# First block of a fused attention and expert kernel: row chunks split in pairs, engine order written by hand

## The chip, the cores and the metric

The kernel runs on 1 core of one Trainium2 chip. The metric is the device time of one execution in microseconds (us). The median of 3 runs of the kernel before is 2581.15 us (2580.57 to 2585.92).

## The reference

The input x is 2 x 2048 tokens of 2048 features. Each token is normalised, and the result goes into an attention layer with one head of width 512 and into a feed-forward layer of 64 gated experts of rank 8; both results are added to x.

```python
xn = _layernorm(x, axis=-1)                       # no weight, no bias
# attention
q, k, v = split(xn @ Wqkv + bqkv)                 # 3 x 512 columns
out_a = softmax(q @ k.T / sqrt(512)) @ v @ Wo + bo
# experts
scores = (xn @ Wq_w.T) @ keys.T                   # 16 router columns, 64 experts
gate = softmax over the 16 greatest scores, 0 elsewhere
z = (xn @ A_w.T) * gate, each gate over its 8 columns
out_f = z @ B_w.T * 2
x = x + out_a + out_f
```

Everything is float32. TensorE multiplies a rounded form (fp32r), so each operand is kept as a high part (the value rounded to fp32r) and a low part (the value minus its high part), and each product is three matmuls: high times high, high times low, low times high.

## The kernel before, in words

Tokens are worked on in blocks of T = 512, a block in NT = 4 rows of 128 tokens; a row's 2048 features are NCH = 16 chunks of 128. The later blocks are read already transposed (xT), are normalised by statistics that were gathered beside other work, and go through matrix products with fewer multiplications (phases P1 to P7). The first block has nothing to hide behind, so it is made from x itself, in `first_block` (L319):

- `load` (L328) reads a row of 128 tokens into two tiles of 128x1024. `normal` (L338) takes four statistics of 512 columns each on VectorE (L225), merges them (L228), makes the negative mean nm (L341) and the variance plus epsilon ve (L218) on VectorE, and 1/sqrt on GpSimd (rs, L219). `scale` (L344) normalises three quarters of the row on VectorE (L349) and the last on ScalarE, in two operations (L353, L354).
- `turn` (L356) transposes the row's 16 chunks on TensorE (L363), four to a PSUM bank, in the banks acc 0, 1, 2 and 6. From each bank ScalarE writes four high parts (`split_hi`, L127) and VectorE four low parts (`split_lo`, L130), chunk by chunk: 128x128 each.
- `piece` and `low` (L396, L399) load the eight pieces of the values' weight wv[0] (two chunks by VH = 264 columns each; 16 of these columns are the router's) and split them: high parts on ScalarE, low parts on VectorE, and on GpSimd for pieces 2, 3 and 4.
- `mul` (L375) multiplies one row by one piece, in 6 matmuls of 128x264, so that a row takes 48. The row's sums lie in the banks acc 3, 4, 5 and 6. Within a product the order of PASSES (L59) is low x with high w, high x with low w, then high with high.
- The loop over the rows t issues `scale` of the row t + 1 ahead of the third piece, `normal` of the row t + 2 behind it, and `turn` of the row t + 1 ahead of the seventh. Then `values_out` (L291) splits the results and stores them, and a second half does the same with wv[1], now piece by piece over all four rows.

The scheduler of the recording layer sets each engine's final order from its own estimates; `behind(...)` (L117) makes an instruction come after a named earlier one of its engine. In the built program VectorE so mixes the rows: statistics of the row t + 2 lie between the low parts of the row t + 1, and weight parts are put in between. On SP's queue stand, in this order: half of row 0, 5 weight pieces, row 1, 3 pieces, rows 2 and 3, six small constants, then the second half's first four pieces and the q weights (wq).

The results of the split, xn, are read twice more: by `features` (L867), which multiplies all chunks with wq (x is then the moving operand, 512 wide), and by `whole` (L1135), which adds high and low parts to the normalised block again, where the next phases need it (L1140, 128x512 each). Where the chunks lie is set by XH0 and XH1 (L178): one 128x1024 slot for each chunk, which holds its high part and its low part; one chunk lies in two half slots. The slots are the later homes of other tiles (GROUPS and T_SLOTS).

TensorE starts with 25 matmuls on zeros in the bank misc, the eighth bank, which later serves small transposes.

Of the kernel before, what the change touches and what calls it, by code (L numbers as in the profile page):

```python
# [62 lines left out]
def attn_ffn_kernel(ctx: ExitStack, tc, x, xT, wq, wv, wob, bqk, bv, bo, keysT, out):  # L63
# [114 lines left out]
    XH0 = [s for n in range(3) for s in (GROUPS[3][n + 1], T_SLOTS[n])] + [26, T_SLOTS[3]]  # L178
    XH1 = [s for n in range(3) for s in (GROUPS[2][n + 1], T_SLOTS[4 + n])] + [None, T_SLOTS[7]]

    def split_room(at):
        if at is None:
            return [half(k)([P, T], FR, "xh") for k in (7, 8)]
        t = big(at)([P, 2, T], FR, "xh")
        return [t[:, k, :] for k in range(2)]
# [133 lines left out]
    def first_block(steps):  # L319
# [3 lines left out]
        xn = [split_room(at) for at in XH0 + XH1]  # L323
        rows, mv = {}, const.tile([P, NT, 2], F32, name="mv", bufs=2)
        rs = const.tile([P, NT], F32, name="rs")
        nm = const.tile([P, NT], F32, name="nm")

# [10 lines left out]
        def normal(t):  # L338
            st = const.tile([P, 4, 6], F32, name="st6", bufs=2)
            row_stats(mv[:, t, :], rows[t], 0, st)  # L340
            last["nm"] = nc.vector.tensor_scalar(nm[:, t : t + 1], mv[:, t, 0:1], -1.0, None, ALU.mult)  # L341
            rstd(rs[:, t : t + 1], mv[:, t, 1:2], 1)

        def scale(t):  # L344
            for n in range(4):
                c, h = divmod(n, 2)
                v = rows[t][c][:, h * 512 : (h + 1) * 512]
                if n < 3:
                    last["row"] = nc.vector.tensor_scalar(  # L349
                        v, v, mv[:, t, 0:1], rs[:, t : t + 1], ALU.subtract, ALU.mult  # L350
                    )
                else:
                    nc.scalar.activation(v, v, AF.Identity, bias=nm[:, t : t + 1])  # L353
                    last["mul"] = nc.scalar.mul(v, v, rs[:, t : t + 1])  # L354

        def turn(t, g0=0, g1=NCH // 4):  # L356
            sl = slice(t * P, (t + 1) * P)
            for g in range(g0, g1):
                pt = acc((0, 1, 2, 6)[g])
                for j in range(4):  # L360
                    c = 4 * g + j
                    k = (c % 8) * P
                    nc.tensor.transpose(pt[:, j * P : (j + 1) * P], rows[t][c // 8][:, k : k + P], ident)  # L363
                for part in range(2):
                    for j in range(4):
                        hi, lo = (xn[4 * g + j][a][:, sl] for a in range(2))
                        pj = pt[:, j * P : (j + 1) * P]
                        if part == 0:
                            split_hi(hi, pj)
                        else:  # L370
                            last["row"] = split_lo(lo, pj, hi)

        r_w0 = Ring(sb, "h0", "h1", "h2", "h3", "B25", "B34", "B35", "B32")

        def mul(ps, wh, t, c2):  # L375
            sl = slice(t * P, (t + 1) * P)
            for cc in range(2):
                c = 2 * c2 + cc
                product(
                    ps[:, :VH], lambda a: xn[c][a][:, sl], lambda b: wh[:, b, cc, :],  # L380
                    c == 0, c == NCH - 1,
                )
# [5 lines left out]
        for j in range(25):  # L388
            nc.tensor.matmul(pw, warm[:, :P], warm, start=True, stop=True)
        load(0, 512)  # L390
        normal(0)
        scale(0)

        wh = []

        def piece():  # L396
            wh.append(wv_hi(0, len(wh), r_w0))

        def low(n):  # L399
            with behind("row", "nm", "mul"):  # L400
                wh[n] = weights_lo(*wh[n], nc.gpsimd if 2 <= n < 5 else None)

        piece()
        piece()
        low(0)
        low(1)
        piece()
        turn(0, 0, 2)
        low(2)
        piece()  # L410
        turn(0, 2, 4)
        low(3)
        piece()
        low(4)
        load(1, 1024)
        for n in range(5, N2):
# [1466 lines left out]
```

## Time and profile before

| what | value |
|---|---|
| median of 3 runs | 2581.15 us (2580.57 to 2585.92) |
| span of the profiled execution | 2582.2 us |
| TensorE busy | 2556.8 us, 99% |
| VectorE busy | 1981.2 us, 77% |
| ScalarE busy | 926.9 us, 36% |
| GpSimd busy | 560.8 us, 22% |
| mean granted TensorE clock | 0.998 |
| DMA | 615.41 MB, mean 238 GB/s |

The page gives the profiled execution by its span, from the first to the last instruction; it has no other time of that execution, so its span stands beside the runs. The profile is of one execution. A group is shown by line, engine and operation, with the tile that it writes, an arrow and the tiles that it reads; "idle before" is the time for which its engine stood still ahead of it, with what ended that. Matmul ends are modelled: starts are the better measure. The clock is a share of full speed.

### The profile page before, as it was taken

To read this page: it belongs to the slowest core of one execution; us is meant where nothing else is said; L and a number is where in the kernel's file an instruction comes from. 1 tells how busy PE (TensorE), PEld (TensorE's weight loads), DVE (VectorE), ACT (ScalarE), POOL (GpSimd) and SP (SyncE) were. 2 spreads that over 40 slices of the span, in tenths; PEclk is the share of its full clock that TensorE was granted. 3 is DMA by queue.
4 is the path that set the end of the run, shared out by engine and by line. 5 is a ranking of instruction groups with operands and counts; after the bars stand their busy time and mean duration, and the time that the engine had idled before them with its cause. 6 is when DMAs were issued, how large, how long until landed. Compare 5 with 4: busy or idle time off the path is not lost. (4 is left out here: it accounts for less than half of the span.)

```text
span 2582.2 us, 34227 instructions
## 1 busy us (share of the span) xinstructions
PE 2556.8 (99%) x12546; PEld 2159.7 (84%) x12546; DVE 1981.2 (77%) x2692; ACT 926.9 (36%) x1327; POOL 560.8 (22%) x340
## 2 busy tenths in 40 slices
PE   9999999999999999999999999999999999999999
PEld 8897888888888889888887878878878888888887
DVE  7788997867778678777668768688597777797675
ACT  4333333232332323343345446354364222332221
POOL 2382310001000000000000000000013565576654
PEclk9999999999999999999999999999999999999999
DMA  8988964668356673678899798898897554665552
GB/s 297 311 300 276 354 224 144 227 212 274 125 176 225 211 250 120 201 269 270 315 310 309 240 338 278 282 324 290 277 320 265 182 162 157 203 200 179 167 168 101
DMA packets 334297, 615.41 MB, mean 238 GB/s; under 512 B 28409, under 2 KB 151345, under 8 KB 334129
## 3 DMA queue, kind: packets, MB, share of 16 engines
q1 hardware_dynamic: 318864, 583.33, 67.2%
q10 hardware_dynamic: 15264, 29.89, 3.3%
q8 instruction: 99, 1.62, 0.3%
q14 instruction: 70, 0.57, 0.1%
HBM read 457.76 MB, written 155.35 MB: 237 GB/s over the span
## 5 line engine op out<-in xcount | busy, mean ns | idle before, releaser
L135 PE MATMUL acc<-t,pw 128*128 128x512 f32 x3744 | 859.0, 390 | 6.4 <-DVE t L130 4.7
L135 PEld LDWEIGHTS acc<-t,pw 128*128 128x128 f32 x3744 | 699.8, 188 | 153.9 <-DVE t L130 6.4
L1629 PE MATMUL acc<-wb,s 128*128 128x512 f32 x2688 | 609.6, 389 | 0.0
L1629 PEld LDWEIGHTS acc<-wb,s 128*128 128x128 f32 x2688 | 504.4, 188 | 105.0 <-DVE s L130 0.2
L1613 POOL TENSOR_TENSOR xo<-xo,bo_bc 128x512 f32<-128x512 f32 x128 | 213.5, 1675 | 884.5 <-DMA bo_bc<-in_bo 592.3
L127 ACT CAST pw<-pw 128x1024 fp32r<-128x1024 f32 (+1 forms) x218 | 230.5, 1058 | 442.1 <-PE acc L135 287.8
L135 PE MATMUL acc<-ph,vt 128*128 128x512 f32 x1536 | 376.7, 390 | 0.3 <-ACT ot L1474 0.2
L130 DVE TENSOR_TENSOR pw<-pw 128x1024 fp32r<-128x1024 f32 (+1 forms) x218 | 288.7, 1324 | 95.9 <-ACT pw L127 94.3
L135 PEld LDWEIGHTS acc<-ph,vt 128*128 128x128 f32 x1536 | 287.7, 188 | 62.1 <-issue 1.2
L1335 PE MATMUL acc<-qt,kt 128*128 128x512 f32 x1344 | 333.9, 390 | 2.6 <-ACT sp L1345 1.5
L1335 PEld LDWEIGHTS acc<-qt,kt 128*128 128x128 f32 x1344 | 250.9, 188 | 58.9 <-DVE qt L130 2.2
L135 PE MATMUL acc<-pw,t 128*128 128x264 f32 x2400 | 295.9, 285 | 2.9 <-DVE pw L130 0.9
L135 PEld LDWEIGHTS acc<-pw,t 128*128 128x128 f32 x2400 | 294.2, 189 | 5.3 <-ACT pw L127 1.1
L127 ACT CAST s<-xz 128x1024 fp32r<-128x1024 f32 x112 | 118.0, 1054 | 375.1 <-PE acc L1629 300.3
L130 DVE TENSOR_TENSOR s<-xz,s 128x1024 fp32r<-128x1024 f32 x112 | 177.8, 1589 | 41.0 <-ACT s L127 41.0
L130 DVE TENSOR_TENSOR t<-xq,t 128x1024 fp32r<-128x1024 f32 x108 | 141.9, 1321 | 24.3 <-ACT t L127 24.1
L535 POOL TENSOR_TENSOR zt<-zt,g 128x512 f32<-128x512 f32 x28 | 44.6, 1603 | 516.0 <-DMA g<-gd 274.6
L127 ACT CAST t<-xq 128x1024 fp32r<-128x1024 f32 x108 | 113.1, 1051 | 114.1 <-DVE xq L667 59.6
L1618 DVE TENSOR_TENSOR xo<-xo,acc 128x512 f32<-128x512 f32 x128 | 86.9, 680 | 52.1 <-POOL xo L1659 25.2
L127 ACT CAST ph<-sp 128x512 fp32r<-128x512 f32 x128 | 79.4, 620 | 109.4 <-PE acc L135 108.5
L1654 POOL TENSOR_TENSOR xo<-xo,u 128x512 f32<-128x512 f32 x64 | 111.5, 1772 | 21.5 <-DVE u L1652 21.4
L225 DVE BATCH_NORM_STATS2 st<-xs 128x6 f32<-128x512 f32 x128 | 85.0, 683 | 39.5 <-DMA xs<-in_x 39.2
(174 smaller groups left out, 2229.4 us busy)
## 6 DMA issues: line engine op xcount, KB each, us to landing
vt<-v_d SPq DMA_DIRECT2D x128, 512.0 KB, 5.4
kt<-kp_d SPq DMA_DIRECT2D x224, 256.0 KB, 5.7
pw<-sq_d SPq DMA_DIRECT2D x96, 512.0 KB, 4.3
pw<-in_wq SPq DMA_DIRECT2D x72, 512.0 KB, 3.7
xo<-in_x SPq DMA_DIRECT2D x128, 256.0 KB, 3.0
xz<-oz_d SPq DMA_DIRECT2D x64, 512.0 KB, 4.4
out_y<-xo SPq DMA_DIRECT2D x128, 256.0 KB, 2.6
xq<-in_xT SPq DMA_DIRECT2D x56, 512.0 KB, 5.1
```

Source lines behind the costliest of these rows:

```text
L127: return nc.scalar.copy(hi, src)
L130: return (eng or nc.vector).tensor_tensor(lo, src, raw(hi), ALU.subtract)
L135: last["pe"] = nc.tensor.matmul(ps, st(a_), mv(b_), start=first and n == 0, stop=end and n == 2, skip_group_check=more,)
L225: nc.vector.bn_stats(st[:, parts, :], xt[:, h * 512 : (h + 1) * 512])
L535: nc.gpsimd.tensor_tensor(zt, zt, gx[n], ALU.mult)
L1335: last["pe"] = nc.tensor.matmul(ps, st[:, d, a, :], mv[c][:, d, :], start=not more and d == 0 and i == 0, stop=d == 1 and i == 2, skip_gro ...
L1613: nc.gpsimd.tensor_tensor(xs, xs, bo_bc[q // (NB // 2 * NH), c], ALU.add)
L1618: nc.vector.tensor_tensor(xs, xs, ps, op)
L1629: nc.tensor.matmul(ps, st[a_][:, kk, sl], mv[b_], start=not more and kk == 0 and n == 0, stop=kk == ND - 1 and n == 2, skip_group_check=more,)
L1654: nc.gpsimd.tensor_tensor(xo[q, t, a, 1], xo[q, t, a, 1], v, ALU.add)
```

## The change

Chunks go in pairs. A slot of 128x1024 now holds the high parts of two neighbouring chunks, or the low parts of two, so that one instruction of 128x2x128 splits two chunks out of a PSUM bank: 8 casts on ScalarE for a row instead of 16, and on VectorE 7 paired subtractions and, for the last pair, whose low parts lie in two half slots, 2 single ones. `whole` adds a pair at a time (128x1024) likewise.

The order in the first half is written out: `inline` puts each instruction behind the one issued before it on its engine (VectorE, ScalarE, TensorE). All loads of the block are issued first; SP's order stays as it was. High parts of the weights follow each bank's casts; low parts of the pieces 2, 4 and 6 are on GpSimd, those of 0, 1, 3, 5 and 7 on VectorE. In `normal` the variance comes ahead of nm. Each product begins with high times high. Transposes of a row's first two banks stand ahead of the previous row's last piece, those of the other two behind it; the fourth bank is misc instead of acc 6.

In the built program VectorE's order is, from the first row's scaling on: low part of piece 0; four chunks; piece 1; four chunks; piece 3; eight chunks; piece 5; statistics of row 1; piece 7; scaling of row 1; twelve chunks of row 1; statistics of row 2; the last four chunks of row 1; scaling of row 2; and so on. ScalarE's, after its first weight cast: the last quarter of row 0 (two operations); piece 1; four chunks; pieces 2 and 3; four chunks; piece 4; four chunks; piece 5; four chunks; pieces 6 and 7; row 1. TensorE's: 16 transposes, 42 matmuls, 8 transposes, 6 matmuls, 8 transposes, 42 matmuls, and so on. Behind the first block the engines' orders are the same but for some neighbouring places between 140 and 210 us, where `whole` stands among other steps.

```diff
-    XH0 = [s for n in range(3) for s in (GROUPS[3][n + 1], T_SLOTS[n])] + [26, T_SLOTS[3]]
-    XH1 = [s for n in range(3) for s in (GROUPS[2][n + 1], T_SLOTS[4 + n])] + [None, T_SLOTS[7]]
+    XH0 = [(GROUPS[3][n + 1], T_SLOTS[n]) for n in range(3)] + [(26, T_SLOTS[3])]
+    XH1 = [(GROUPS[2][n + 1], T_SLOTS[4 + n]) for n in range(3)] + [(T_SLOTS[7], None)]
...
+        def inline(key, f, *a, **k):
+            if key in tail:
+                with tc.issue_after(tail[key].ins):
+                    tail[key] = f(*a, **k)
+            else:
+                tail[key] = f(*a, **k)
+            return tail[key]
...
         def normal(t):
             st = const.tile([P, 4, 6], F32, name="st6", bufs=2)
-            row_stats(mv[:, t, :], rows[t], 0, st)
-            last["nm"] = nc.vector.tensor_scalar(nm[:, t : t + 1], mv[:, t, 0:1], -1.0, None, ALU.mult)
-            rstd(rs[:, t : t + 1], mv[:, t, 1:2], 1)
+            for k in range(4):
+                c, h = divmod(k, 2)
+                dve(nc.vector.bn_stats, st[:, k, :], rows[t][c][:, h * 512 : (h + 1) * 512])
+            dve(nc.vector.bn_aggr, mv[:, t, :], st)
+            ve = const.tile([P, NT], F32, name="ve", bufs=2)
+            dve(nc.vector.tensor_scalar, ve[:, :1], mv[:, t, 1:2], EPS, None, ALU.add)
+            nc.gpsimd.tensor_tensor(rs[:, t : t + 1], ve[:, :1], nhalf[:, :1], ALU.pow)
+            dve(nc.vector.tensor_scalar, nm[:, t : t + 1], mv[:, t, 0:1], -1.0, None, ALU.mult)
...
+        def turn(t, g):
+            pt = turned[t, g] = acc(g) if g < 3 else misc()
+            for j in range(4):
+                c = 4 * g + j
+                k = (c % 8) * P
+                pe(nc.tensor.transpose, pt[:, j * P : (j + 1) * P], rows[t][c // 8][:, k : k + P], ident)
+
+        def sides(t, g, part):
+            sl = slice(t * P, (t + 1) * P)
+            for cp in (2 * g, 2 * g + 1):
+                src = turned[t, g][:, (cp % 2) * 2 * P : (cp % 2 + 1) * 2 * P]
+                src = src.rearrange("p (k t) -> p k t", k=2)
+                hi, lo = xn[cp]
+                if part == 0:
+                    act(split_hi, hi[:, :, sl], src)
+                elif isinstance(lo, list):
+                    for k in range(2):
+                        dve(split_lo, lo[k][:, sl], src[:, k, :], hi[:, k, sl])
+                else:
+                    dve(split_lo, lo[:, :, sl], src, hi[:, :, sl])
...
+                for n, (a, b) in enumerate(PASSES[::-1]):
...
+        wload(5)
+        load(1, 1024)
+        wload(3)
+        load(2, 1024)
+        load(3, 1024)
+        normal(0)
+        high()
         scale(0)
-        wh = []
-        def piece():
-            wh.append(wv_hi(0, len(wh), r_w0))
-        def low(n):
-            with behind("row", "nm", "mul"):
-                wh[n] = weights_lo(*wh[n], nc.gpsimd if 2 <= n < 5 else None)
...
+        high()
         low(0)
+        for g in range(4):
+            turn(0, g)
+            sides(0, g, 0)
+            sides(0, g, 1)
+            high()
+            if g == 0:
+                low(1)
+                high()
+            if g == 1:
+                low(2)
+                low(3)
+            if g == 3:
+                low(4)
+                low(5)
+                high()
+        low(6)
+        constants()
+        ps = [acc(3 + t) for t in range(NT)]
         for t in range(NT):
-            ps.append(acc(3 + t))
             for c2 in range(N2):
-                if t + 1 < NT and c2 == 2:
-                    scale(t + 1)
-                    if t + 2 < NT:
-                        with behind("row"):
-                            normal(t + 2)
-                if t == 0 and c2 == 4:
-                    low(6)
-                    low(7)
-                    load(3, 1024)
-                    constants()
-                if t + 1 < NT and c2 == 6:
-                    with behind("pe"):
-                        turn(t + 1)
+                if t + 1 < NT and c2 == 0:
+                    normal(t + 1)
+                    if t == 0:
+                        low(7)
+                    else:
+                        sides(t, 3, 1)
+                    scale(t + 1)
+                if t + 1 < NT and c2 == N2 - 1:
+                    turn(t + 1, 0)
+                    turn(t + 1, 1)
                 mul(ps[t], wh[c2], t, c2)
+            if t + 1 < NT:
+                for g in range(4):
+                    if g > 1:
+                        turn(t + 1, g)
+                    sides(t + 1, g, 0)
+                    if g < 3 or t + 2 == NT:
+                        sides(t + 1, g, 1)
...
     def whole(ch, cp):
         t = big(GROUPS[3 - ch][cp])([P, 2, T], F32, "xq")
-        for k in range(2):
-            hi, lo = xn[ch * HC + 2 * cp + k]
-            nc.vector.tensor_tensor(t[:, k, :], raw(hi), raw(lo), ALU.add)
+        hi, lo = xn[(ch * HC) // 2 + cp]
+        if isinstance(lo, list):
+            for k in range(2):
+                nc.vector.tensor_tensor(t[:, k, :], raw(hi[:, k, :]), raw(lo[k]), ALU.add)
+        else:
+            nc.vector.tensor_tensor(t, raw(hi), raw(lo), ALU.add)
```

## Prediction

> **What bounds the kernel now.** I read the page first, then TensorE's timeline over the first 45 us, then VectorE's, then busy time and granted clock in stretches.
>
> ```profile
> span 2582.2 us, 34227 instructions
> ...
> PE 2556.8 (99%) x12546; PEld 2159.7 (84%) x12546; DVE 1981.2 (77%) x2692; ACT 926.9 (36%) x1327; POOL 560.8 (22%) x340
> ```
>
> TensorE has work 99% of the time; over the whole span it is idle for 2582.2 - 2556.8 = 25.4 us. A change that keeps its matmuls can only win idle time, and time at a low clock. The change touches the first block, so I look there (TensorE; start, length, group, idle before):
>
> ```profile
> 9.29 1.91 PE L363 MATMUL acc<-ident,xs 128*128 128x128 f32 x16
> 12.01 3.31 PE L135 MATMUL acc<-wh,xh 128*128 128x264 f32 x25 [0.81 <-DVE xh L130]
> 15.63 1.00 PE L135 MATMUL acc<-wh,xh 128*128 128x264 f32 x6 [0.31 <-POOL wh L130]
> 18.51 0.88 PE L135 MATMUL acc<-wh,xh 128*128 128x264 f32 x5 [1.89 <-DVE wh L130]
> 19.52 2.98 PE L363 MATMUL acc<-ident,xs 128*128 128x128 f32 x16
> 22.15 0.57 PE L135 MATMUL acc<-wh,xh 128*128 128x264 f32 x1
> 23.00 6.33 PE L135 MATMUL acc<-wh,xh 128*128 128x264 f32 x47 [0.28 <-DVE xh L130]
> 29.17 1.91 PE L363 MATMUL acc<-ident,xs 128*128 128x128 f32 x16
> 30.83 6.09 PE L135 MATMUL acc<-wh,xh 128*128 128x264 f32 x48
> 36.77 1.91 PE L363 MATMUL acc<-ident,xs 128*128 128x128 f32 x16
> 38.43 1.71 PE L135 MATMUL acc<-wh,xh 128*128 128x264 f32 x12
> 41.52 3.68 PE L135 MATMUL acc<-wh,xh 128*128 128x264 f32 x28 [1.38 <-DVE xh L130]
> ```
>
> From start to start, 16 transposes take 30.83 - 29.17 = 1.66 us (0.104 each) and 48 matmuls 36.77 - 30.83 = 5.94 (0.124 each): 7.60 us a row of tokens. The first half of the values so ends at 41.52 + 48 x 0.124 = 47.45. The waits sum to 0.81 + 0.31 + 1.89 + 0.28 + 1.38 = 4.67 us. VectorE stands behind nearly all of them:
>
> ```profile
> 11.66 3.26 DVE L130 TENSOR_TENSOR xh<-acc,xh 128x128 fp32r<-128x128 f32 x16 [0.86 <-ACT xh L127]
> 14.84 2.46 DVE L225 BATCH_NORM_STATS2 st<-xs 128x6 f32<-128x512 f32 x4
> 17.33 0.26 DVE L228 BATCH_NORM_AGGREGATE mv<-st 128x2 f32<-128x24 f32 x1
> 17.63 0.15 DVE L341 TENSOR_SCALAR nm<-mv 128x1 f32<-128x1 f32 x1
> 17.70 0.14 DVE L218 TENSOR_SCALAR ve<-mv 128x1 f32<-128x1 f32 x1
> 17.76 0.70 DVE L130 TENSOR_TENSOR wh<-ws,wh 128x528 fp32r<-128x528 f32 x1
> 18.91 1.46 DVE L349 TENSOR_SCALAR xs<-xs,mv,rs 128x512 f32<-128x512 f32 x3 [0.46 <-POOL rs L219]
> ```
>
> From the second row's first statistics (14.84) to its scaling (18.91) are 4.07 us, and 0.61 more to its first transpose. The stretches (TensorE's busy time is the first after the colon, the clock follows POOL) show the price of the hole at 16.6 to 18.5:
>
> ```profile
> 16.86:20.27 3.41, 1.63 (x12) 1.37 (x13) 2.88 (x8) 1.51 (x3) 0.96 (x1) 1.00 0.75 276
> 20.27:23.68 3.41, 3.13 (x16) 2.80 (x15) 3.41 (x11) 3.27 (x17) 0.22 (x1) 0.51 0.78 232
> ```
>
> TensorE was busy for 1.63 of 3.41 us, and the next 3.41 us had half the clock: 1.7 us lost.
>
> **The change part by part.** *Paired splits.* A row has 16 high casts on ScalarE and 16 subtractions on VectorE; now 8 casts, and 7 paired plus 2 single subtractions. Neither trace row is 2x128 wide. ScalarE: 2.81 / 16 = 0.176 for one of 128; a 128x256 copy out of PSUM later in the trace takes 0.38 alone, less the 0.10 by which neighbours overlap (a cast of 128 lasts 0.28 to 0.33): 0.28. Bounds 0.25 and 2 x 0.176 = 0.35. VectorE: 2.85 / 14 = 0.204 for 128, 1.05 / 3 = 0.35 for 248; I take 0.36, bounds 0.35 and 2 x 0.204 = 0.41 (above it lies the 512-wide row, 0.68 alone, some 0.61 in a chain). A row: ScalarE 8 x 0.28 = 2.24 for 2.81, VectorE 7 x 0.36 + 2 x 0.204 = 2.93 for 3.25.
>
> [...]
>
> *Row 0.* SP's loads stand in the same order, so statistics end as before; the variance now goes ahead of nm: scaling 0.08 earlier, 8.03 to 9.49. On ScalarE the row's last quarter is scaled before the second weight cast, which ends near 9.92. Then by the built order, with 0.58 per weight cast (1.16 / 2): high pairs at 9.92, two weight casts, pairs at 11.64, a cast, pairs at 12.78, a cast, pairs at 13.92. VectorE must see both casts of a bank: 0.28 + 0.38 = 0.66 after each of these starts. Its chain, 0.65 a weight subtraction (1.32 / 2): weight 0 to 10.14; wait to 10.58, two pairs to 11.28; weight 1 to 11.93; wait to 12.30, pairs to 13.0; weight 3 to 13.65, pairs to 14.35; wait to 14.58, a pair and two singles to 15.33; weight 5 to 15.98. Only then come the second row's statistics: 15.98 for 14.84, since two weight subtractions (1.3) stand ahead of them and the pairing repays little. The first transpose of row 1 so comes at 15.98 + 4.07 + 0.61 - 0.08 = 20.6 us (before 19.52).
>
> *TensorE meanwhile.* High times high goes first, so its start at 11.2 replaces 12.01; it follows the pieces (13.7 for piece 3, 16.0 for piece 5) and has done 42 matmuls by 17.5; the order by hand now puts the transposes next. It stands 3.1 us: one hole instead of two. I let the following 3.4 us run at half clock as the row shows: from 20.6 to 23.7, 1.6 us lost.
>
> [...]
>
> *Rows 1 to 3.* What is left at 20.6: 48 transposes and 150 matmuls, 48 x 0.104 + 150 x 0.124 = 23.6 us. Is VectorE quick enough? From a row's first transpose: third bank at 0.83 + 0.74 = 1.57, its subtractions at 1.57 + 0.63 (transpose to cast, 37.40 - 36.77) + 0.66 = 2.86, done 3.56; the next row's statistics to 6.02; variance and GpSimd's power 1.23 (GpSimd 0.55 beside PSUM work), in which the last bank's 0.76 are hidden; scaling and first transpose 0.6: 7.85. TensorE needs 7.60, so 0.25 is lost at each of two rows. End: 20.6 + 23.6 + 1.6 + 0.5 = 46.3, say 46.2 with roundings. Before: 47.45. **Gain 1.25 us.** The eighth bank (misc) costs nothing: its old readers, the casts and subtractions of the row before, are done 5 us ahead. The waits of 1.38 at the last row and 0.28 go; what is late next is the scaling.
>
> *The second half* begins at 46.2. Its first weight cast follows the last row's casts at about 43.3 (before 42.56), its subtraction ends near 44; needed at 46.2. SP's wq loads that wait for row 3's slots, and the v_d and weight loads queued behind them, come up to 1.5 us later, while the need is 1.2 earlier. The tightest piece is subtracted by 61.2 and needed at 65.2: 4 us less 2.7 leave it hidden; without that cover each microsecond late is one lost.
>
> *Features.* xn's slots change their content; TensorE's instructions do not. Rebuilding rows takes 7 x 1.21 + 2 x 0.64 = 9.75 us of VectorE for 16 x 0.64 = 10.24, beside a busy TensorE: nothing. Near 200 us the weight subtraction that TensorE waits for (1.72 us at 204.3) moves ahead of one 0.42 us operation: 0.15 taken, bounds 0 and 0.42.
>
> Sum: -1.25 - 0.15 = -1.4. The page gives the profiled execution's span alone, 2582.2, which lies 1.05 above the median 2581.15 of runs from 2580.57 to 2585.92. 2582.2 - 1.4 = 2580.8, less 1.05: **2579.7 us**.
>
> **Rivals.** *Given back* (0.22): between 150 and 300 us TensorE is idle for 1.13 + 4.74 + 1.45 = 7.3 us behind VectorE, which has waited for DMA. If that chain keeps its time, the gain ends there: 2581.2. For it: DMA shares of 0.87 to 0.95 from 50 to 200. Against: most of its issues follow TensorE's progress.
> *More than forecast* (0.16): no slow clock (-1.6), and half of those 7.3 us vanish with the new order: 2579.7 - 1.6 - 3.6 = 2574.5. Against: nothing removes work there.
> *Slower* (0.15): the paired subtraction with its strided ends costs more than two single ones. Each 0.1 above 0.36 adds 0.7 to the start of row 1 and to each of two loops, 2.1 in all; from 0.42 the block loses. At 0.61, the 512-wide row's, it ends 5.2 later, and holes of 2 us a row bring another slow stretch (1.7): 2579.7 + 6.9 = 2586.6. For it: VectorE is the bound, no row shows the form. Against: 128 and 248 lie on one line.
> That the order does not come out is excluded by the built program.
>
> **Chances.** Forecast 0.47, given back 0.22, more 0.16, slower 0.15. A measurement tells about 0.2% (5.2 us) from no change: below 2576.0 lies most of "more", 0.14; above 2586.3 most of "slower", 0.11; within 0.75. Range from near the one to near the other: 2575.0 to 2585.5.
>
> **What would show it.** One TensorE hole of about 3 us before row 1's transposes near 20.6, a half clock behind it, no wait over 0.5 later, the first half's end near 46.2, 2x128 subtractions at 0.36 a step, VectorE without a rest. Wrong if the end lies beyond 47.5 or before 44.5, or if the stage at 195 to 262 moves by more than a microsecond against the start.

## The result, and the profile after

| | before | changed |
|---|---|---|
| median of 16 runs each | 2583.15 us (2580.17 to 2586.44) | 2587.64 us (2580.16 to 2592.32) |
| profiled execution: span | 2582.2 us | 2584.3 us (its time 2586.1) |
| mean granted clock, profiled execution | 0.998 | 0.997 |

The changed kernel takes 1.0016 times as long, 95% interval [1.0009, 1.0022], about 4 us more where a gain of 1.4 us, to 2579.7 us, was forecast. A second set of runs gave 1.0018 [1.0009, 1.0027].

Two lines of the page of the changed kernel (span; busy time, share and instructions of each engine):

```profile
span 2584.3 us, 34175 instructions
...
PE 2559.1 (99%) x12546; PEld 2161.9 (84%) x12546; DVE 1975.9 (76%) x2657; ACT 924.2 (36%) x1295; POOL 546.7 (21%) x340
```

VectorE lost 35 instructions and 5.3 us, ScalarE 32 and 2.7 us: the change did what it says. TensorE did not get its work sooner. Its timeline in the first block (start, length, group, idle before and its releaser):

```profile
10.97 1.10 PE L338 MATMUL acc<-wh,xh 128*128 128x264 f32 x7
13.09 3.48 PE L338 MATMUL acc<-wh,xh 128*128 128x264 f32 x24 [1.02 <-DVE wh L130]
17.36 1.60 PE L338 MATMUL acc<-wh,xh 128*128 128x264 f32 x11 [0.79 <-DVE wh L130]
21.95 1.74 PE L338 MATMUL acc<-ident,xs 128*128 128x128 f32 x8 [3.00 <-issue]
...
31.47 1.13 PE L338 MATMUL acc<-ident,xs 128*128 128x128 f32 x8
...
39.44 1.13 PE L338 MATMUL acc<-ident,xs 128*128 128x128 f32 x8
...
41.93 18.26 PE L338 MATMUL acc<-wh,xh 128*128 128x264 f32 x148
```

One hole of 3.0 us stands ahead of row 1's transposes, as forecast, but it ends at 21.95 instead of 20.6. The last row's matmuls start at 41.93, so the first half ends at 41.93 + 48 x 0.124 = 47.9: 0.4 later than before, not 1.25 earlier. VectorE in that time, and then GpSimd:

```profile
5.48 1.88 DVE L338 BATCH_NORM_STATS2 st<-xs 128x6 f32<-128x512 f32 x3 [0.40 <-DMA xs<-in_x]
...
11.26 1.78 DVE L130 TENSOR_TENSOR wh<-ws,wh 128x528 fp32r<-128x528 f32 x1
12.96 0.74 DVE L130 TENSOR_TENSOR xh<-acc,xh 128x256 fp32r<-128x256 f32 x2
13.62 1.16 DVE L130 TENSOR_TENSOR wh<-ws,wh 128x528 fp32r<-128x528 f32 x1
14.71 0.74 DVE L130 TENSOR_TENSOR xh<-acc,xh 128x256 fp32r<-128x256 f32 x2
15.37 0.80 DVE L130 TENSOR_TENSOR xh<-misc,xh 128x256 fp32r<-128x256 f32 x3
16.10 1.21 DVE L130 TENSOR_TENSOR wh<-ws,wh 128x528 fp32r<-128x528 f32 x1
17.23 2.46 DVE L338 BATCH_NORM_STATS2 st<-xs 128x6 f32<-128x512 f32 x4
```

```profile
11.15 1.32 POOL L130 TENSOR_TENSOR wh<-ws,wh 128x528 fp32r<-128x528 f32 x1 [2.29 <-ACT wh L127]
12.77 1.45 POOL L130 TENSOR_TENSOR wh<-ws,wh 128x528 fp32r<-128x528 f32 x1 [0.29 <-ACT wh L127]
15.41 1.33 POOL L130 TENSOR_TENSOR wh<-ws,wh 128x528 fp32r<-128x528 f32 x1 [1.19 <-ACT wh L127]
```

The paired subtractions take 0.37 each. But VectorE's weight subtractions, priced at 0.65, took 1.78, 1.16 and 1.21 wherever one of GpSimd's ran at the same time. Statistics of row 1 start at 17.23 instead of 15.98.

Part of that was lost earlier. In the kernel before, the same load was waited for until 5.52, but only two of the four statistics were left then:

```profile
5.52 1.29 DVE L225 BATCH_NORM_STATS2 st<-xs 128x6 f32<-128x512 f32 x2
```

Row 0 comes in quarters, two on SP's queue and two on ScalarE's. By the waits in the trace the kernel before takes SP's first, ScalarE's first, SP's second, ScalarE's second. The new loop in `normal` takes both of SP's first and so waits for SP's second while ScalarE's first is there: three statistics are left instead of two, and scaling starts at 8.60 instead of 8.11 (8.03 was forecast). It starts at 8.47 to 9.06 in all 12 profiles with the changed first block, and at 7.95 to 8.51 in the four with the old one.

The larger part of the loss in the profiled execution is far behind. I compared the starts of TensorE's small matmuls in the bank misc, which stand at the same place in both programs: the changed kernel is 0.44 us late at 76 us, 3.74 at 180, 4.19 at 235, 2.76 at 281 and 2.48 at 1199. The 3.3 us come in one wait, here in the changed kernel and then in the one before:

```profile
165.48 18.14 PE L135 MATMUL acc<-pw,t 128*128 128x264 f32 x135 [3.38 <-ACT yv L997]
```

```profile
162.09 8.14 PE L135 MATMUL acc<-pw,t 128*128 128x264 f32 x63 [0.47 <-ACT yv L941]
```

ScalarE's copies yv, which empty the bank, are queued behind its cast of a value-weight tile, and that waits for the tile's load (yv starts at 165.06, before at 161.67):

```profile
162.19 1.07 ACT L127 CAST pw<-pw 128x1056 fp32r<-128x1056 f32 x1 [4.47 <-DMA pw<-in_wv]
```

The load is late because the queue of SP (SyncE) is late. It stood still here (columns of the waits: us in total, times, longest); the first line is of the changed kernel, the second of the one before:

```profile
SPq L1228 <- DVE xq L1199: 10.1, 1, 10.1
```

```profile
SPq L1169 <- DVE xq L1140: 3.3, 1, 3.3
```

SP was to load a part of the query weights (hs) into a slot that the last rebuilding add of `whole` has to free first. The changed kernel's VectorE and GpSimd at that place:

```profile
126.78 3.87 DVE L1199 TENSOR_TENSOR xq<-xh 128x1024 f32<-128x1024 f32 x3
130.56 2.32 DVE L130 TENSOR_TENSOR t<-xq,t 128x1024 fp32r<-128x1024 f32 x1
132.81 2.35 DVE L130 TENSOR_TENSOR pw<-pw 128x1056 fp32r<-128x1056 f32 x1
135.08 2.31 DVE L1199 TENSOR_TENSOR xq<-xh 128x1024 f32<-128x1024 f32 x1
...
139.54 0.68 DVE L588 TENSOR_TENSOR zt<-acc,g 128x512 f32<-128x512 f32 x1
```

```profile
130.34 1.46 POOL L597 TENSOR_TENSOR hs<-hs 128x512 f32<-128x512 f32 x1 [15.92 <-DMA hs<-in_wq]
131.88 2.16 POOL L598 TENSOR_TENSOR hs<-hs 128x512 f32<-128x512 f32 x1
```

From 130 us on the operations of both engines are longer. VectorE's take 2.3 us instead of 1.2 and start 2.25 and 2.27 apart (130.56, 132.81, 135.08); GpSimd's next three take 2.15 to 2.19 and start 2.24 and 2.26 apart (131.88, 134.12, 136.38), where the same sums take 1.29 and 1.30 from 152.87 on, while VectorE stands idle. I read this as the two engines taking turns, one operation each. The add ends at 137.4. In the kernel before VectorE ran through (0.61 us an add), the last add ended at 130.6, and GpSimd's first sum was held (a length of 6.38):

```profile
125.70 4.89 DVE L1140 TENSOR_TENSOR xq<-xh 128x512 f32<-128x512 f32 x8
130.52 1.24 DVE L130 TENSOR_TENSOR pw<-pw 128x1056 fp32r<-128x1056 f32 x1
...
133.96 0.67 DVE L532 TENSOR_TENSOR zt<-acc,g 128x512 f32<-128x512 f32 x1
```

```profile
128.82 6.38 POOL L541 TENSOR_TENSOR hs<-hs 128x512 f32<-128x512 f32 x1 [15.47 <-DMA hs<-in_wq]
```

The add is not SP's only wait for VectorE. Behind it stands the store of zt (the expert products times their gates), and behind that the next value-weight load; in the changed kernel:

```profile
SPq L170 <- DVE zt L588: 1.9, 1, 1.9
```

```profile
140.24 0.33 SPq L170 DMA_DIRECT2D oz_d<-zt  x1
```

The start of zt is the better mark of how late SP's queue is: from zt to yv it is 25.0 to 26.3 us in all 12 profiles with the changed first block (27.7 in the kernel before), while the end of the last add lies anywhere from 27 to 33 us ahead of yv. From the first add to zt VectorE took 8.26 us before and 12.76 in the changed kernel.

Last, the clock. The profile's clock records know full speed and half, and half comes in stretches of 3.41 us (3.413 in the records of both profiles; only the last stretch, at the end of the span, has another length, 3.89 and 0.75), which a window of 5 us shows as about two thirds. In the profiled execution of the changed kernel such stretches follow the 3.00 and 3.38 us waits, and a third one the wait of 2.98 us that ends at 229.6 (us, length, busy time of PE, PEld, DVE, ACT and POOL, clock, DMA share, GB/s):

```profile
20.00:25.00 5.00, 3.05 (x15) 3.08 (x16) 3.64 (x10) 2.74 (x6) 1.02 (x1) 0.72 0.86 269
25.00:30.00 5.00, 5.00 (x42) 5.00 (x41) 3.58 (x9) 1.20 (x4) 0.00 (x0) 0.94 0.66 259
165.00:170.00 5.00, 4.52 (x24) 4.52 (x25) 5.00 (x3) 3.29 (x7) 4.92 (x3) 0.66 1.04 404
230.00:235.00 5.00, 5.00 (x16) 3.51 (x15) 4.96 (x5) 0.00 (x0) 4.84 (x3) 0.66 0.02 8
```

One such stretch costs 1.7 us. Runs without a profile have a mean clock, given to 0.001: in the second set (1 - clock) x span was on average 6.3 us for the changed kernel and 5.2 for the one before, 1.2 of the 3.8 us between their means.

### The profile page after: what moved, and what is told of

It is laid out like the page before. It is cut to its first block, busy times and chain, and to the rows that moved or that the text cites. A ratio compares the mean times of both kernels' runs of the same rounds, so it can differ in the third digit from the quotient of the medians.

```text
span 2584.3 us, 34175 instructions
## 1 busy us (share of the span) xinstructions
PE 2559.1 (99%) x12546; PEld 2161.9 (84%) x12546; DVE 1975.9 (76%) x2657; ACT 924.2 (36%) x1295; POOL 546.7 (21%) x340
## 5 line engine op out<-in xcount | busy, mean ns | idle before, releaser
L1672 POOL TENSOR_TENSOR xo<-xo,bo_bc 128x512 f32<-128x512 f32 x128 | 208.3, 1634 | 890.7 <-DMA bo_bc<-in_bo 590.2
L1404 ACT COPY sp<-acc 128x512 f32<-128x512 f32 x128 | 74.6, 584 | 105.3 <-PE acc L1394 105.1
```

The source lines that it names most:

```text
L1404: last["copy"] = nc.scalar.copy(*ops)
L1672: nc.gpsimd.tensor_tensor(xs, xs, bo_bc[q // (NB // 2 * NH), c], ALU.add)
```

## The experiments

My theory after the comparison: GpSimd's and VectorE's operations with both inputs in SBUF take turns, which eats the first block's gain and, at 127 to 140 us, makes SP late; long waits of TensorE cost a stretch of half clock on top. The restriction to SBUF is read from the changed kernel's trace: two paired subtractions out of a PSUM bank took 0.74 us at 12.96, beside a subtraction of GpSimd's (12.77 to 14.22), and 0.76 at 26.51, with GpSimd idle. Rivals: the order of VectorE behind the first block alone (a split and a weight subtraction ahead of the last add); or the first block alone. The experiments stand in the order in which they ran; the first four still test the order. A ratio is to the kernel before on the same chip; "late" is TensorE's start near the named time against the kernel before's profiled execution.

**together**: changed kernel, the four rebuilding adds kept together (held_back issues a step behind a named earlier instruction, here the last add of whole).

```diff
-        10: [L[1]] + b0 + q_[2:3],
+        10: [L[1]] + b0 + [lambda: held_back(q_[2])],
...
```

> The changed kernel, with the four additions that rebuild the first half of the normalised block kept next to one another on VectorE: the second group's split now waits for the last of them. Theory A (the loss is SP's queue: the last addition, put behind a split and a weight subtraction, lets slot 26 free 7 us late, SP's weight loads stand behind the hs load that waits for that slot, and TensorE waits 3.4 us at 165 us and drops its clock): hs loads in one stretch near 125 to 131, no TensorE wait above 1 us near 165, the transpose at 180 us no later than 0.6 us against before, time within 0.05% of before (ratio 0.9995 to 1.0005). Theory B (the loss is the first block itself, its 3 us hole and what the clock makes of it): unchanged, ratio near 1.0016. Theory C (the new content of the slots, high pairs and low pairs, makes features slower): unchanged too, and the delay grows between 70 and 140 us.

2584.03 us, 1.0007 [0.9998, 1.0016]. SP's wait for the add fell from 10.1 to 5.4 us, but GpSimd still came in between, and SP then stood for zt instead (5.9 us for 1.9):

```profile
127.22 6.24 DVE L1199 TENSOR_TENSOR xq<-xh 128x1024 f32<-128x1024 f32 x4
133.38 2.35 DVE L130 TENSOR_TENSOR pw<-pw 128x1056 fp32r<-128x1056 f32 x1
135.65 4.54 DVE L130 TENSOR_TENSOR t<-xq,t 128x1024 fp32r<-128x1024 f32 x2
140.12 0.68 DVE L588 TENSOR_TENSOR zt<-acc,g 128x512 f32<-128x512 f32 x1
```

```profile
SPq L170 <- DVE zt L588: 5.9, 1, 5.9
```

The adds ended 4 us sooner, at 133.5, and nothing came of it: 12.90 us from the first add to zt, yv at 165.40, 2.48 us of wait at 165.8, TensorE 4.09 late at 180 (the changed kernel 3.74). The median lies lower than the changed kernel's, but the two intervals overlap, so that the order has a part is not shown.

**apart**: kernel before, the split put among the adds.

```diff
-        10: [L[1]] + b0 + q_[2:3],
+        10: [L[1]] + b0[:3] + q_[2:3] + b0[3:],
```

> The kernel before, first block and slots untouched; only the last of the four additions (two instructions here) is issued behind the second group's split, so that VectorE's and SP's orders near 130 us are those of the changed kernel. Theory A: slower by 2 to 5 us, ratio 1.0008 to 1.002, SP waiting some 7 to 10 us for the addition, a TensorE wait of 2 us or more near 162. Theories B and C: no change, ratio within 0.0005 of 1.

2582.66 us, 1.0003 [0.9994, 1.0012]. SP waited 5.4 us instead of 3.3, not the 7 to 10 expected, and TensorE at 161 us only 0.17. Here GpSimd's first sum was held for 4.62 us, and from the first add to zt it was 9.35 us. The order alone does not cost the 4 us; the theory of the order falls. (The profiled execution lost time later, by a wait of 4.25 us at 228.6.)

**stats_early**: together, with row 1's statistics ahead of two weight subtractions.

```diff
                 low(4)
+                low(6)
+                normal(1)
                 low(5)
                 high()
-        low(6)
...
-                    normal(t + 1)
-                    if t == 0:
-                        low(7)
-                    else:
+                    if t:
+                        normal(t + 1)
                         sides(t, 3, 1)
                     scale(t + 1)
+                    if t == 0:
+                        low(7)
```

> As the first kernel of this set, and in the first block the second row's statistics go ahead of the low part of weight piece 5, and the low part of piece 7 behind that row's scaling. If VectorE's chain sets the second row's first transpose, that transpose comes 0.8 us earlier than the 21.95 of the changed kernel (21.0 to 21.3), the hole of 3.0 us ahead of it splits in two, and the first half ends 0.6 to 0.9 us earlier, near 47.1; time 0.7 us under the first kernel of this set, which a measurement can hardly tell. If something else sets it (DMA, GpSimd), it does not move.

2584.16 us, 1.0008 [0.9999, 1.0017]. The statistics went ahead, but row 1's transposes came at 22.8 all the same, not at 21.0 to 21.3: TensorE then waited 3.19 us at 20.4 for the weight subtraction that had been moved back.

**filled**: together, with zeros multiplied in the hole.

```diff
+                if t == 0 and c2 == N2 - 1:
+                    idle = acc(0)
+                    for j in range(12):
+                        pe(nc.tensor.matmul, idle, warm[:, :P], warm, start=True, stop=True)
                 if t + 1 < NT and c2 == N2 - 1:
                     turn(t + 1, 0)
```

> As the first kernel of this set, and TensorE fills its hole ahead of the second row's transposes with 12 matmuls on zeros (bfloat16, 128x512, some 0.21 us each, 2.6 us in all) into a bank that is overwritten afterwards. If the hole is what halves the clock behind it: clock 1.0 between 20 and 27 us, the two groups of transposes in 0.83 us instead of 1.39, the first half's end 1.2 to 1.7 us earlier (46.2 to 46.7), mean granted clock up by 0.0006, time 1 to 2 us under the first kernel of this set. If the clock falls for another reason, the end stays at 47.9.

2584.91 us, 1.001 [1.0002, 1.0019]. The clock stayed at 1.0 from 20 to 27 us and the last row's matmuls began at 40.2 instead of 41.9: the half clock is worth its 1.7 us in the block. It was given back: 0.06 us early at 99, 0.51 late at 180, 3.83 at 235. Waits stood at 50.3 (1.04 us), 162.9 (1.30) and here:

```profile
228.28 11.02 PE L135 MATMUL acc<-t,pw 128*128 128x512 f32 x35 [4.78 <-DVE t L130]
```

There VectorE's subtraction t is queued behind statistics that wait for x's loads.

**after_again**: the changed kernel unaltered, beside the next three.

> The changed kernel once more, unaltered, beside the three that follow. Theory of the order (late in the first block's wake the rebuilding adds make SyncE's queue late, and TensorE waits at 165 us for the cast of the value weights): 2586 to 2588 us again, with a wait of 3.4 us at 165 us and a stretch of half clock behind it. Theory of the clock (the first block is no faster, and each wait of over 2.5 us costs another 1.7 us at half clock): the same time, and the runs with the lower granted clock are the longer ones.

2585.89 us, 1.0018 [1.0009, 1.0027]; TensorE waited 2.45 us at 165.7, with half clock behind it.

**orders_alike**: together, the rebuilding adds 512 columns wide again.

```diff
-        if isinstance(lo, list):
-            for k in range(2):
-                nc.vector.tensor_tensor(t[:, k, :], raw(hi[:, k, :]), raw(lo[k]), ALU.add)
-        else:
-            nc.vector.tensor_tensor(t, raw(hi), raw(lo), ALU.add)
+        for k in range(2):
+            low = lo[k] if isinstance(lo, list) else lo[:, k, :]
+            last["whole"] = nc.vector.tensor_tensor(t[:, k, :], raw(hi[:, k, :]), raw(low), ALU.add)
```

> The changed first block, its slots of high and low parts kept, but each rebuilding add 512 columns wide as before the change and the first query-weight split held behind the last of them, so that behind the first block every engine but TensorE has the order that it had before. Theory of the order: SyncE's wait near 130 us falls from 10.1 to about 3.3 us, TensorE's at 165 us from 3.4 to about 0.5 us, and the time is 2582 to 2583.5 us, with only the first block's own +0.4 us left. Theory of the first block: TensorE still waits over 2 us near 165 us, because what feeds it there is late from the first block on, and the time stays at 2584 or above.

2590.28 us, 1.003 [1.0019, 1.0042]: the theory of the order missed. That of the first block has the sign (2584 or above) but not the size, since most of the loss came later (1.9 late at 99, 4.3 at 180, 8.2 at 235). The expectation is wrong on the order too: a weight subtraction stood ahead of the last of the eight adds. The seven before it took 5.80 us, since a sum of GpSimd's (131.35, 1.30) ran among them; the same short adds had not let it in before. From the first add to zt it was 13.05 us. TensorE waited 3.42 us at 166.9 and 2.30 at 211.6. So narrow adds do not repair the changed kernel; how much of the further loss is theirs is open, since the order differs from that of together too.

**no_gpsimd_splits**: orders_alike, all low parts of the first block's weights on VectorE.

```diff
-            if n in (2, 4, 6):
-                split_lo(wh[n][:, 1], ws[n], wh[n][:, 0], nc.gpsimd)
-            else:
-                dve(split_lo, wh[n][:, 1], ws[n], wh[n][:, 0])
+            dve(split_lo, wh[n][:, 1], ws[n], wh[n][:, 0])
```

> The kernel before this one (orders alike), with the three low parts of weights that GpSimd computes in the first block put on VectorE too. Theory of contention (VectorE's weight subtractions took 1.2 to 1.8 us instead of 0.65 because GpSimd's ran beside them): every weight subtraction on VectorE takes about 0.65 us, six or seven of them 4 to 4.6 us in all, and the second row's statistics start within 0.5 us of the 17.2 us that they had with GpSimd's help; so GpSimd's share was worth next to nothing, and the time is within 1.5 us of orders alike. Rival (VectorE's were slow for another reason, the strided target or the load): they stay at 1.2 us or more, the statistics start at 19 us or later, and the time is 2 us longer.

VectorE's timeline:

```profile
11.13 0.70 DVE L130 TENSOR_TENSOR wh<-ws,wh 128x528 fp32r<-128x528 f32 x1
...
12.73 1.32 DVE L130 TENSOR_TENSOR wh<-ws,wh 128x528 fp32r<-128x528 f32 x2
...
15.49 1.94 DVE L130 TENSOR_TENSOR wh<-ws,wh 128x528 fp32r<-128x528 f32 x3
17.34 2.47 DVE L338 BATCH_NORM_STATS2 st<-xs 128x6 f32<-128x512 f32 x4
```

With GpSimd out of the way each takes 0.65 to 0.70, and the statistics start at 17.34. With GpSimd's help they started at 17.23 in the changed kernel and at 17.77 in orders_alike, of which this is the variant: against the one three subtractions on GpSimd saved 0.1 us, against the other they cost 0.4. 2588.7 us, 1.003 [1.0018, 1.0041], like orders_alike.

**filled_ahead**: orders_alike, the zeros of filled, and the second half's next weight piece ahead of the statistics.

```diff
+        nxt = wv_piece(1, 0)
         for c2 in range(N2):
-            w = wv_piece(1, c2)
+            w, nxt = nxt, wv_piece(1, c2 + 1) if c2 + 1 < N2 else None
...
```

> Orders alike, with 12 more matmuls of zeros (into a bank that is overwritten later; the output is unchanged) ahead of the second row's transposes, and the second half's next weight piece subtracted ahead of the statistics that wait for x. Theory of the clock and of the waits: no half clock at 20 to 27 us, no wait at 51 us, the second half ends 1.5 to 2 us sooner than in orders alike; then the gain is kept past 99 us, and the time is 2580 to 2581.5 us if it also passes 165 and 228 us, or within 0.5 us of before if the loads and statistics at these two places take it back, each with a longer wait there. The theory that the first block's gain is always absorbed downstream expects the second, with waits of 1.5 us or more at 163 us and over 4 us at 228 us.

2591.73 us, 1.0033 [1.0021, 1.0046]. No half clock and, from row 1 on, no wait before 99 us, where TensorE is 0.44 early; 6.5 late at 186, 9.1 at 244. Half clock held for 10.2 us from 163. Both expected times were missed: the early start was more than given back.

**after_no_sums** and **before_no_sums**: GpSimd's four sums of the second weight part left out, in either kernel. If turns are the cause, VectorE's operations there are back at 1.2 us in the changed kernel and TensorE's wait at 165 us shrinks, while the kernel before, where the first sum was held, gains nothing.

```diff
     def part_sums(n):
-        held["part", n] = four_sums(*(held[n, "part", fh, ch] for fh in range(2) for ch in range(2)))
+        parts = [held[n, "part", fh, ch] for fh in range(2) for ch in range(2)]
+        held["part", n] = four_sums(*parts) if n != 1 else [parts[k] for k in (3, 0, 2, 1)]
```

> The changed kernel without GpSimd's four sums of the second weight part (the four operations that ran from 130 to 138 us beside VectorE's adds and splits); the unsummed parts are stored instead, so this kernel leaves work out and its output is not the reference's. [...] Rival (the first block alone makes everything late): VectorE is faster but TensorE still waits over 2 us at 165 us, and the time stays at 2585 to 2587 us.

> The same four sums left out of the kernel before (the output is not the reference's). [...] Rival (less work on GpSimd helps either kernel alike): it gains as much as the changed kernel gains, 2 us or more.

The changed kernel without the sums: 2582.88 us, 1.0004 [0.9996, 1.0013]. Its VectorE and SP's wait:

```profile
132.03 1.22 DVE L130 TENSOR_TENSOR t<-xq,t 128x1024 fp32r<-128x1024 f32 x1
133.17 1.25 DVE L130 TENSOR_TENSOR pw<-pw 128x1056 fp32r<-128x1056 f32 x1
134.34 1.22 DVE L1199 TENSOR_TENSOR xq<-xh 128x1024 f32<-128x1024 f32 x1
...
136.83 0.68 DVE L588 TENSOR_TENSOR zt<-acc,g 128x512 f32<-128x512 f32 x1
```

```profile
SPq L1228 <- DVE xq L1199: 6.0, 1, 6.0
```

The same three operations take 1.2 instead of 2.3 us, it is 8.58 us from the first add to zt instead of 12.76, yv starts at 162.50, and the wait at 165 us is gone: 1.47 us late at 100, 0.53 at 180, 0.06 early at 235. (SP's wait for the add is 6.0 us all the same.) The kernel before without them: 2581.8 us, 1.0001 [0.9992, 1.0009], with VectorE from 125 to 134 unchanged to 0.2 us, though its profiled execution was 2.0 us early at 1199 us. So the sums cost the kernel before nothing that its runs show, and the changed kernel some 3 us (1.0004 against 1.0016 and 1.0018, which come from other sets of runs and whose intervals meet). That GpSimd's sums make VectorE's operations there longer (2.3 us beside them, 1.2 without) is thereby the cause of the larger part; the path from it to the wait at 165 us is read from the traces.

**wide_filled_ahead**: together, with the zeros and the piece ahead.

> The changed kernel with three edits: the first query-weight split held behind the last rebuilding add (as in together), 12 matmuls of zeros ahead of the second row's transposes (as in filled; the output is unchanged), and the second half's next weight piece subtracted ahead of the statistics that wait for x. Rebuilding adds stay 1024 wide. Theory that the first block's gain is real and lost downstream: no half clock at 20 to 27 us, no wait at 51 us, TensorE 1.5 to 2 us ahead of the changed kernel at 99 us; then waits at 163 and 228 us that are together at least as much longer, and 2582 to 2585 us in the end. If the gain is kept it is 2580 to 2581.5 us.

2586.78 us, 1.002 [1.0012, 1.0029]. 0.53 us early at 98 (the block's gain is real), then GpSimd among the adds (four in 6.11 us), waits of 2.94 us at 165 and 5.49 at 232: 3.30 late at 183, 7.09 at 242, and a time above the expected 2582 to 2585.

**before_filled**: the kernel before with the zeros.

```diff
+                if t == 0 and c2 == 6:
+                    idle = misc()
+                    with behind("pe"):
+                        for j in range(12):
+                            nc.tensor.matmul(idle, warm[:, :P], warm, start=True, stop=True)
```

> The kernel before with the same 12 matmuls of zeros ahead of its second row's transposes (the output is unchanged). Theory of absorption: the half clock at 20 to 24 us goes, the first block ends up to 1.5 us sooner, and the time is within 1 us of before, because TensorE waits longer at 162, 204 or 226 us. Rival (a microsecond won in the first block is a microsecond won): 2580 to 2581 us, with milestones past 235 us 1 us or more earlier.

2584.21 us, 1.0016 [1.0007, 1.0026]. The half clock at 20 to 25 us was gone and the last row's matmuls still began 0.45 later (41.97 for 41.52); half clock came at 205 and 229 instead. Neither expectation held. The zeros did not fit the gap: they began at 19.03, and row 1's transposes at 21.63 behind them instead of 19.52, so that this run does not show what an earlier end of the block is worth. It does show that a kernel with nothing late by more than half a microsecond at 99 us can take as much longer as the changed one.

**loads_later**: the changed kernel, complete, with the second weight part's loads one place later on SP's queue (issued behind zt). If turns are the cause, sums that start later leave VectorE's adds alone for longer.

```diff
-                nc.vector.tensor_tensor(zt, ps, gx[n], ALU.mult)
+                last["zt"] = nc.vector.tensor_tensor(zt, ps, gx[n], ALU.mult)
...
-        10: [L[1]] + b0 + q_[2:3],
-        11: [S_[1]] + q_[3:] + [L[2]],
+        10: b0 + q_[2:3],
+        11: q_[3:] + [lambda: held_back(L[1], "zt"), S_[1], L[2]],
...
```

> The changed kernel, complete, with one edit: the loads of the second weight part stand one place later on SyncE's queue (behind the next value-weight load instead of ahead of it), so that they land about 3 us later and GpSimd's sums start near 133 instead of 130.3 us. [...] Rival (the sums' start is not what counts, only their number): the sums slow VectorE as much wherever they start, SyncE waits over 9 us, and the time stays at 2586 to 2588 us.

2584.01 us where the kernel before took 2583.89: 1.0001 [0.9992, 1.001]. GpSimd began at 134.45 instead of 130.34; VectorE's split and subtraction ran at 1.22 and 1.25, only the last add at 2.32; SP waited 6.9 us. The last add ended at 137.6, no sooner. With all the work kept it was 10.56 us from the first add to zt for 12.76: when the two engines meet counts, not only the work. But the profile does not show the chain at 165 us repaired. TensorE came 3.51 us late from the first half (two stretches of half clock, a wait of 1.54 at 53.8), VectorE's adds began 2.4 us later than in the changed kernel, and yv at 164.79, only 0.27 sooner; there is no wait there because TensorE was late itself (3.09 at 180).

**loads_later_filled**: the same in wide_filled_ahead, whose lead at 98 us may so last past 165.

> The same edit in wide_filled_ahead (12 matmuls of zeros, next weight piece ahead of the statistics, first query-weight split behind the last rebuilding add). [...] Rival as above: 2586 to 2588 us again.

2587.06 us, 1.001 [1.0002, 1.0019]. Its profiled execution (2584.2 us) was 0.63 us early at 98, 0.51 at 179 and 0.42 at 1198, with 0.98 us of wait at 162; but the runs spread from 2582 to 2593, and their median is that of the rival. No version here beats the kernel before.

## Why the prediction was wrong

The change was forecast at -1.4 us and came out at +4.5 between the medians. Another 2.0 us of the distance to 2579.7 are the base: I worked from three runs at 2581.15, and the 16 runs of the same kernel have 2583.15. I also set the span 2582.2 beside run times, but a run's time lies some 1.8 us above its span (2586.1 and 2584.3 in the profiled execution of the changed kernel); the forecast starts from the median and does not change by that. By terms:

- **Paired splits** held: 0.36 to 0.38 a pair on VectorE for 0.36, 0.30 to 0.34 on ScalarE for 0.28.
- **Row 0** failed, at two places. "Statistics end as before" overlooked the order of the quarters: scaling began at 8.60 for 8.03. And "0.65 a weight subtraction" was 1.2 to 1.8 beside GpSimd's: from start to start three of them took 3.92 us for 1.95, against which 1.04 us of waits for ScalarE that I had counted did not come. Of the first transpose's 1.35 us of delay (21.95 for 20.6) 0.57 are the first and 0.68 the second, the chain from scaling to row 1's statistics (8.63 for 7.95). The trace of before had the row for the second, on GpSimd:

```profile
9.92 3.34 POOL L130 TENSOR_TENSOR wh<-ws,wh 128x528 fp32r<-128x528 f32 x2 [1.55 <-ACT wh L127]
```

The first took 2.05 us, begun beside VectorE's two weight subtractions (9.48 to 10.80); the second, beside VectorE's subtractions out of PSUM, 1.33. I put both engines side by side at full speed. The runs show for a weight subtraction on VectorE 1.2 to 1.8 us beside one of GpSimd's, 0.65 to 0.70 without (no_gpsimd_splits).
- **TensorE meanwhile** held: one hole of 3.0 us, then 3.41 us at half clock.
- **Rows 1 to 3** held but for their start: 7.97 us from row to row for 7.85, and no wait later.
- **The second half** held in the profiled execution; in after_again and in several variants one piece near 52 us was late by 0.9 to 1.5 us. I had left 1.3 us of cover to another one, needed at 65.2, as the tightest.
- **Features** failed, and with it the sign: rebuilding "beside a busy TensorE: nothing" was wrong. SP's queue stands for what VectorE does there, for the slot that the last add frees and for zt, with TensorE's value weights behind both. That stretch took 12.76 us instead of 8.26 because GpSimd's sums fell into it, and TensorE waited 3.38 us at 165.5 for 0.47 before. I had priced VectorE's own time, 9.75 for 10.24 us, and not what GpSimd would add to it. VectorE's order differs from 126 us on, not from 140. The 1.72 us at 204 did shrink to 0.71, but it was bought by coming 2.75 us later.
- The range was too narrow: no rival let the stage at 165 us lose, and three runs were a thin base. The rival "slower" named 2586.6, near the outcome, by luck: its cause, a paired subtraction at 0.61 us, did not occur. Two signs of being wrong came true: the first half ended at 47.9, beyond 47.5, and the stage at 195 to 262 moved (TensorE 0.46 late at 99, 3.74 at 191, 2.76 at 281).

What stays open: when GpSimd gets in. It was held for 6.38, and in apart 4.62 us by VectorE's run of operations, but ran at once among the same kind of adds in orders_alike. In the filled kernels I did not separate why an earlier first block ends later. And the milestones are of one profiled execution each: after_again's was 3.99 late at 180 and yet ended with a span of 2580.6 us, under that of the kernel before (2582.2), so they show where time is lost, not how much of it is left at the end.

## What to carry to other kernels

Price an elementwise operation by what the other engine does at that moment: where VectorE and GpSimd both read two SBUF tiles, sharing work saved next to nothing here (three subtractions on GpSimd moved the statistics from 17.34 to 17.23 in one kernel and to 17.77 in the other). An instruction off the critical path is not free if a queue waits for it: look for what it frees or stores, and for what stands behind that in the queue. When an order that a scheduler made is written out by hand, compare the two orders instruction by instruction; here the quarters of one row cost 0.5 us. A wait that got shorter proves nothing while the next one in the same queue takes it up. And a gain at the start of a kernel that is fed by loads is only a gain where every later stage has slack; compare milestones, not only the changed stage.

## What the runs showed of the hardware

- Elementwise operations with both inputs in SBUF, beside each other and alone, in the changed kernel: VectorE (128x1024) 2.3 us from 130.56 and 1.21 at 122.23, GpSimd (128x512) 2.16 us at 131.88 and 1.30 at 152.87.
- TensorE's waits of 3.0 to 3.4 us from 19, 162 and 227 us were each followed by 3.41 us at half clock (from 22.18, 165.54 and 230.40) in the changed kernel's profiled execution. The prediction let a hole of 3.1 us cost 1.6 us at half clock, by the row at 16.86 alone; the hole of 3.0 us had its stretch. Shorter ones came ahead of such stretches too: two of 0.90 us at 1287 and 1289 us before, one of 1.55 at 1388 in the changed kernel. And a long one can go free: 3.42 us at 166.9 in orders_alike, 3.25 at 226.3 in after_no_sums.
- Over the 16 profiles half clock went with how busy TensorE had been in a window of a fixed grid (by its records, whose ends are modelled). Within a profile all half-clock stretches lie on one grid of 3.41 us: before, they start 372 and 750 such steps behind the first at 20.33, in the changed kernel 42, 61 and 401 behind the first at 22.18. Of the grid's windows at full clock, between 8 us and the last 20, those in which TensorE was busy for less than 0.48 were followed by half clock in 33 of 33 cases, those between 0.48 and 0.56 in 6 of 26, and those above in none of some 11,850. In the profile before, the windows from 1286.7 and 16.9 us, busy for 0.472 and 0.495, were followed by half clock, and those from 225.1, 201.2 and 1385.7 us, for 0.484, 0.495 and 0.549, were not; in the changed kernel's the four that were had 0.02, 0.12, 0.22 and 0.55, and the next in order had 0.65. The 3.42 us of orders_alike fell into two windows, busy for 0.51 and 0.48.
